# Transposed copies of x and adj loaded in 32x32 blocks, and attention's products with v issued in pairs

## The chip, the cores and the metric

The kernel runs on one core of a Trainium2 chip. The metric is the device time of one execution in microseconds (us). TensorE (PE in the profile, its weight loads PEld), VectorE (DVE), ScalarE (ACT), GpSimd (POOL) and SyncE (SP) each run their own instructions in order; 16 DMA engines move data. Here DMAs are issued by SP and, in a few places, by ACT.

## The reference

32 independent graphs, each with x[512, 256] and a 0/1 matrix adj[512, 512], pass through four layers. In all of them `x = layernorm(x + layer(x, adj))`.

```
layer 0: q, k, v = x@Wq+bq, x@Wk+bk, x@Wv+bv          (8 heads of 32)
         s = q @ k.T / sqrt(32); s = where(adj > 0, s, -9e15)
         out = (softmax(s) @ v) @ Wo + bo
layer 1: relu(((1+eps)*x + adj@x) @ W1 + b1) @ W2 + b2              (hidden 512)
layer 2: silu(rmsnorm((eps*x + adj@x) @ W1 + b1)) @ W2 + b2         (hidden 1024)
layer 3: softplus(xn@W_self + (I - s_out*adj*s_in) @ xn @ W_neigh), xn = layernorm(x)*gamma + beta
```

`s_out` and `s_in` are the inverse square roots of adj's column and row sums. All is float32.

## The kernel before

**The planner.** `graph(b)` does not issue instructions. It notes operations: an engine, a cost in ns, a function that issues the instructions, the tiles read and written. `Order` (L53 to L261) then makes one list of all 32 graphs' operations. It runs a model in which each engine takes, among the operations that could start soonest, the one with the smallest due time (`run`, L100); a graph's due times are shifted by `PERIOD` for each graph (`emit`, L240). `slot_time` (L135) keeps an operation back until its buffers are free: each tile tag has a fixed number of buffers. A DMA from SP occupies the queue for its `issue` time and lands `lat` (2000 by default) after its cost. The functions are called in the list's order, so the order on each engine is fixed before the program runs; the model's costs have no other effect. Two graphs overlap: the late layers of one run beside the attention of the next.

**Loads and transposes.** For each graph SP loads x (`xs`, one buffer, L374) and adj (`ad`, one buffer, L377) with rows on partitions. Matrix products need both with the other axis on partitions. TensorE transposes 128x128 blocks into PSUM: 16 for adj (L556; ACT copies the result to `adjT`, two buffers, and sums the out-degrees on the way, L563), 8 for x (L585; VectorE or ACT copies to `xT`, one buffer, L590). `bias` (bfloat16, L573) is 0 where adj is set and a huge negative number elsewhere. `adjT` is used from the first aggregation (L1037) to the Laplacian (L1299); its diagonal is kept in `diag0` (L952) and altered for layers 1 and 2. The row sums `d_in` are made by VectorE from `ad` (L964).

**Attention** (`attend`, L666). Heads go in two groups of four. For each of four row tiles of 128 queries:

- TensorE forms the scores of four heads (row-tiled products, L680) in PSUM.
- Per head, VectorE adds `bias`, negates, takes the row minimum, and writes to `pr` (three buffers, L699); ACT computes the exp of `pr` into `pq` (two buffers, L713), in a permuted order of columns, with the row sum.
- VectorE transposes all 32x32 blocks of `pq` in place (128x2048, L728).
- 16 DMAs of 64 KB move quarters of partitions to `pT` (two buffers, L739). SP issues them; in the first graph ACT shares them.
- TensorE multiplies with v, 32 column-tiled products (`pv`, L777) into `po_att`, one quarter of its columns per row tile.

A group ends by scaling with the reciprocal row sums (L796 to L848). The other layers are products (L863, L1037, L1054, L1258, L1299) with elementwise work between them.

Of the kernel before, what the change touches and what calls it, by code (L numbers as in the profile page):

```python
# [11 lines left out]
AF = mybir.ActivationFunctionType  # L12
ALU = mybir.AluOpType
# [3 lines left out]
P = 128  # L17
NEG = -9007199254740992.0
LN_EPS = 1e-5
RMS_EPS = 1e-6  # L20
HEADS = 8
PERIOD = 70000
LEAD = {}


# [27 lines left out]
class Order:  # L53
# [46 lines left out]
    def run(self, ops, key, back=False):  # L100
# [32 lines left out]
        done, out = set(), []  # L133

        def slot_time(o):  # L135
            t = 0.0
            for x in o.bufs:
                if not x.taken:
                    s = slots.setdefault(x.slot, [0.0] * x.bufs)
                    if not s:  # L140
                        return None
                    t = max(t, min(s))
            return t

        while len(out) < len(ops):
            best = None
            for e, lst in cand.items():
# [3 lines left out]
                for c in lst:  # L151
# [4 lines left out]
                    t = max(free[e], o.ready, st)  # L156
                    way = o.ways[c[3]]
                    if e == "DVE" and "port" in way[3] and pool_busy[0] <= t < pool_busy[1]:
                        t = pool_busy[1]
# [18 lines left out]
                x = min((x for x in opts if x[0] <= t_min + self.WINDOW), key=lambda x: x[1])  # L178
# [8 lines left out]
            t, e, c = best  # L187
# [22 lines left out]
            for x in o.bufs:  # L210
                if not x.taken:
                    x.taken = True
                    s = slots[x.slot]
# [51 lines left out]
def kernel(  # L265
# [29 lines left out]
    nc = tc.nc  # L295
    B, N, D = x.shape
    NT = N // P
    DC = D // P
    HD = D // HEADS
    HPG = P // HD  # L300
# [11 lines left out]
    ident = const.tile([P, P], F32, name="ident")  # L312
# [167 lines left out]
    def graph(b):  # L480
        first, last = b == 0, b == B - 1
        def op(ways, r=(), w=(), hold=()):
            order.op(b, ways, r, w, hold, stage[0])
# [3 lines left out]
        def bank(name):  # L487
            return Buf(ps, [P, 512], F32, "m", f"{name}_{b}", 4)

        def tmp(shape, tag, bufs, name=None, dtype=F32):  # L490
            return Buf(sb, shape, dtype, tag, f"{name or tag}_{b}", bufs)

        def pe(cost, fn, r, w, *hold, turn="whole"):

            op([("PE", cost, fn, {"turn": turn})], r, w, hold)

        def dve(cost, fn, r, w, port=False):
            op([("DVE", cost, fn, {"port": 1} if port else {})], r, w)
# [10 lines left out]
        def evacuate(dst, src, r, w):  # L509
            either(  # L510
                r, w,
                (690, lambda: nc.vector.tensor_copy(dst(), src())),
                (590, lambda: nc.scalar.copy(dst(), src())),
            )
# [17 lines left out]
        def small(name, bufs=2, shape=None):  # L532
            return Buf(sb, shape or [P, NT], F32, "s_" + name, f"{name}_{b}", bufs)
# [12 lines left out]


        stage[0] = "adjT"
        adjT = tmp([P, NT, N], "adjT", 2)
        d_out, d_in = small("d_out"), small("d_in")  # L550
        for m in range(NT):
            pt = bank("pt_adj")

            def tr_adj(m=m, pt=pt):
                for t in range(NT):
                    nc.tensor.transpose(  # L556
                        pt[:, t * P : (t + 1) * P], ad[:, t, m * P : (m + 1) * P], ident
                    )

            pe(460, tr_adj, [(ad,)], [(pt,)], adjT, d_out)  # L560
            act(
                675,
                lambda m=m, pt=pt: nc.scalar.activation(  # L563
                    adjT[:, m, :], pt(), AF.Identity, accum_out=d_out[:, m : m + 1]
                ),
                [(pt,)], [(adjT, m), (d_out, m)],
            )
        allT = [(adjT, m) for m in range(NT)]

        bias = tmp([P, NT, N], "bias", 1, dtype=BF16)  # L570
        dve(
            1250,
            lambda: nc.vector.tensor_scalar(  # L573
                bias(), ad(), scalar1=0.0, scalar2=NEG, op0=ALU.is_le, op1=ALU.mult
            ),
            [(ad,)], [(bias,)], port=True,
        )
        stage[0] = "xT"
        xT = tmp([P, DC, N], "xT", 1)
        for c in range(DC):  # L580
            pt = bank("pt")

            def tr_x(c=c, pt=pt):
                for t in range(NT):
                    nc.tensor.transpose(  # L585
                        pt[:, t * P : (t + 1) * P], xs[:, t, c * P : (c + 1) * P], ident
                    )

            pe(460, tr_x, [(xs,)], [(pt,)], xT)
            evacuate(lambda c=c: xT[:, c, :], pt, [(pt,)], [(xT, c)])  # L590
        y = tmp([P, NT, D], "y_att", 2)
        pool(
            2400,
# [10 lines left out]
        def qk(m):  # L604
            stage[0] = "qk"
            for w, w_k, dst, bias_c, bias_k, scale in (
                (wq, "wq", qT, bqs_c, "bqs_c", QK_SCALE),
                (wk, "wk", kT, bk_c, "bk_c", 1.0),
            ):
                pq = bank("pq")  # L610

                def mm(w=w, pq=pq):
                    for c in range(DC):
                        nc.tensor.matmul(  # L614
                            pq(),
                            lhsT=w[:, c, m * P : (m + 1) * P],
                            rhs=xT[:, c, :],
                            start=(c == 0),
                            stop=(c == DC - 1),
                        )  # L620

                pe(1720, mm, xTc + [(w_k,)], [(pq,)], dst)
                col = bias_c[:, m : m + 1]
                either(
                    [(pq,), (bias_k,)], [(dst, m)],
                    (
                        750,
                        lambda dst=dst, pq=pq, col=col, scale=scale: nc.vector.tensor_scalar(
                            dst[:, m, :], pq(), scalar1=scale, scalar2=col,
                            op0=ALU.mult, op1=ALU.add,  # L630
                        ),
                    ),
                    (
                        680,
                        lambda dst=dst, pq=pq, col=col, scale=scale: nc.scalar.activation(
                            dst[:, m, :], pq(), AF.Identity, bias=col, scale=scale
                        ),
                    ),
                )
# [26 lines left out]
        def attend(g):  # L666
# [2 lines left out]
            mx = small("mx", 2, [P, NT, HPG])  # L669
            rs = small("rsum", 2, [P, NT, HPG])  # L670
            po = bank("po_att")
            for t in range(NT):
                stage[0] = "scores"

# [18 lines left out]
                pq = tmp([P, 4, HPG, NT, 32], "pq", 2)  # L693
                for j in range(HPG):

                    pr = tmp([P, N], "pr", 3)
                    dve(
                        780,
                        lambda t=t, j=j, sc=sc, pr=pr: nc.vector.tensor_tensor_reduce(  # L699
                            out=pr(),  # L700
                            in0=sc[:, j, :],
                            in1=bias[:, t, :],
                            scale=-1.0,
                            scalar=3.0e38,
                            op0=ALU.add,
                            op1=ALU.min,
                            accum_out=mx[:, t, j : j + 1],
                        ),
                        [(sc, j), (bias,)], [(pr,), (mx, t, j)],
                    )  # L710
                    act(
                        800,
                        lambda t=t, j=j, pr=pr, pq=pq: nc.scalar.activation(  # L713
                            pq[:, :, j].rearrange("p a c s -> p c a s"),
                            pr().rearrange("p (c a s) -> p c a s", a=4, s=32),
                            AF.Exp,
                            bias=mx[:, t, j : j + 1],
                            scale=-1.0,
                            accum_out=rs[:, t, j : j + 1],
                        ),  # L720
                        [(mx, t, j), (pr,)], [(pq, j), (rs, t, j)],
                        table="exp",
                    )
                stage[0] = "move"
# [6 lines left out]
                    ),  # L731
                    [], [(pq, j) for j in range(HPG)], port=True,
                )
                pT = tmp([P, 4, HPG, NT, 32], "pT", 2)

                def move(queue, to, pq=pq, pT=pT):
                    for a in to:
# [24 lines left out]
                else:  # L762
# [5 lines left out]
                        pqk, [(pT, a) for a in range(4)],  # L768
                    )

                stage[0] = "pv"
                def pv(t=t, pT=pT):

                    for c in range(NT):
                        for j in range(HPG):
                            h = g * HPG + j
                            nc.tensor.matmul(  # L777
                                po[j * HD : (j + 1) * HD, t * P : (t + 1) * P],
                                lhsT=v[:, c, h * HD : (h + 1) * HD],
                                rhs=pT[:, :, j, c, :],  # L780
                                start=(c == 0),
                                stop=(c == NT - 1),
                            )

                pe(
                    1060, pv, [(pT, a) for a in range(4)] + [(v, c) for c in range(NT)],
                    [(po,)], oT, turn="col",
                )

# [622 lines left out]
```

## Time and profile before

| | |
|---|---|
| median of 3 runs | 3604.89 us (3603.01 to 3605.39) |
| profiled execution: its time, its span | 3604.95 us, 3603.2 us |
| granted TensorE clock, mean | 0.989 |
| PE busy | 3501.9 us (97%), 20616 products |
| VectorE busy | 2902.0 us (81%) |
| ScalarE busy | 1836.2 us (51%) |
| GpSimd busy | 854.7 us (24%) |
| DMA engines' time, SP's queue | 36.5%, 253440 packets |
| DMA engines' time, ACT's queue | 0.4%, 2304 packets |
| moves `pT<-pq` from SP | 4048 of 64 KB, 2.0 us to landing |
| loads of adj, of x | 32 of 1024 KB, 5.8 us; 32 of 512 KB, 4.0 us |

A line of a group gives the kernel line, engine, operation, output and inputs by the program's names, shapes, count; then busy us and the mean ns of one; then the idle time just before and what ended it. A line of waits gives who waited for whom, us in total, how often, the longest. A line of the chain gives start, length, and what ran or was waited for; the chain is followed back from the last instruction.

### The profile page before, as it was taken

How to read it: one execution, taken by the hardware profiler on the slowest of the kernel's cores; microseconds unless marked ns; L12 is line 12 of the kernel's file. 1: busy time of each engine (PE TensorE's matmuls, PEld its weight loads, DVE VectorE, ACT ScalarE, POOL GpSimd, SP SyncE). 2: the span in 40 equal slices, each digit the busy share in tenths (PEclk: the TensorE clock that was granted, in tenths of full speed). 3: DMA queues.
4: the chain of work that ended last, by engine and by line, in shares of the span. 5: the costliest groups of instructions: out<-in, count | busy, mean ns of one | idle time of the engine just before them, and what ended most of it. 6: DMA issues, size and time to landing. Idle time of an engine off the chain costs nothing.

```text
span 3603.2 us, 60546 instructions
## 1 busy us (share of the span) xinstructions
PE 3501.9 (97%) x20616; PEld 2086.9 (58%) x20616; DVE 2902.0 (81%) x6458; ACT 1836.2 (51%) x3591; POOL 854.7 (24%) x614
## 2 busy tenths in 40 slices
PE   6899999999999999999999999999999999999897
PEld 3455565665565665555655555655656655656464
DVE  6778888888888888887888888888888888887855
ACT  3445554545554545555455555455545455544533
POOL 1112222222222122222122222122222222221221
PEclk8999999999999999999999999999999999999998
DMA  6434333334333333333333333343333343333410
GB/s 174 115 91 109 93 99 100 94 88 106 98 102 97 91 96 101 99 100 93 94 99 98 100 99 95 92 101 100 98 99 95 87 106 99 101 97 79 100 30 12
DMA packets 256052, 344.82 MB, mean 96 GB/s; under 512 B 71552, under 2 KB 107776, under 8 KB 255744
## 3 DMA queue, kind: packets, MB, share of 16 engines
q1 hardware_dynamic: 253440, 337.79, 36.5%
q10 hardware_dynamic: 2304, 3.15, 0.4%
q8 instruction: 165, 2.70, 0.3%
q14 instruction: 143, 1.17, 0.1%
HBM read 55.46 MB, written 16.78 MB: 20 GB/s over the span
## 4 chain that ended last, share of the span: by engine, by line
PE 82%; ACT 5%; SPq 5%; DVE 2%; issue 2%; DMA 1%; ACTq 0%; POOL 0%; DVEq 0%; POOLq 0%
PE po L863 21%; PE ph L1037 11%; PE pg L1054 10%; PE sc L680 6%; PE pa L1054 6%; PE pz L1258 6%; PE pq L614 6%; PE pa_l L1299 6%; SPq L739 5%; PE po_att L777 5%; PE pv L650 3%; ACT L1349 1%; PE pt L585 1%; PE pt L1230 1%; PE pt_adj L556 1%
## 5 line engine op out<-in xcount | busy, mean ns | idle before, releaser
L713 ACT ACTIVATE pq<-pr,mx 128x512 f32<-128x512 f32 x1024 | 729.0, 713 | 437.6 <-DVE mx L699 203.9
L699 DVE CUSTOM_DVE_ANT_0 pr<-sc,bias 128x512 f32<-128x512 f32 x1024 | 665.0, 684 | 205.2 <-PE sc L680 172.7
L728 DVE STREAM_TRANSPOSE pq<-pq 128x2048 f32<-128x2048 f32 x256 | 590.5, 2307 | 41.9 <-ACT pq L713 30.6
L863 PE MATMUL po<-w,gT 128*128 128x256 f32 x2048 | 478.6, 385 | 5.2 <-ACT gT L1193 5.2
L1054 PE MATMUL pg<-hT,w 128*128 128x512 f32 x1024 | 470.8, 599 | 2.2 <-DVE gT L1109 1.1
L863 PEld LDWEIGHTS po<-w,gT 128*128 128x128 f32 x2048 | 387.0, 191 | 111.7 <-issue 54.9
L916 POOL TENSOR_TENSOR rstd<-ve,nhalf 128x4 f32<-128x4 f32 x132 | 132.4, 1003 | 1286.4 <-DVE ve L911 1280.5
L520 POOL TENSOR_TENSOR ssq<-ssq,sq 128x512 f32<-128x512 f32 x219 | 279.4, 1276 | 211.8 <-ACT sq L1130 205.1
L1054 PEld LDWEIGHTS pg<-hT,w 128*128 128x128 f32 x1024 | 187.1, 190 | 235.0 <-issue 212.7
L777 PE MATMUL po_att<-pT,v 128*32 128x128 f32 x8192 | 281.2, 279 | 32.7 <-DMA pT<-pq 22.7
L680 PE MATMUL sc<-kT,qT 32*128 32x512 f32 x2048 | 298.1, 652 | 9.2 <-DVE mx L699 9.2
L777 PEld LDWEIGHTS po_att<-pT,v 128*32 128x32 f32 x8192 | 211.7, 110 | 157.2 <-issue 119.2
L1037 PE MATMUL ph<-adjT,y 128*128 128x512 f32 x512 | 242.9, 599 | 0.1
L1037 PE MATMUL ph<-adjT,y_att 128*128 128x512 f32 x512 | 239.8, 593 | 0.9 <-DVE y L877 0.9
L1054 PE MATMUL pa<-hT,w 128*128 128x512 f32 x512 | 236.3, 605 | 0.0
L863 PE MATMUL po<-w,aT 128*128 128x256 f32 x1024 | 234.6, 382 | 0.0
L1258 PE MATMUL pz<-wsn,xnT 128*128 128x512 f32 x512 | 230.8, 602 | 0.9 <-DVE xnT L1241 0.4
L1299 PE MATMUL pa_l<-zy,adjT 128*128 128x256 f32 x1024 | 227.6, 380 | 1.3 <-DVE zy L1310 1.3
L1299 PEld LDWEIGHTS pa_l<-zy,adjT 128*128 128x128 f32 x1024 | 194.1, 190 | 42.7 <-issue 15.3
L863 PEld LDWEIGHTS po<-w,aT 128*128 128x128 f32 x1024 | 189.7, 190 | 46.2 <-issue 21.9
L563 ACT ACTIVATE adjT<-pt_adj 128x512 f32<-128x512 f32 x128 | 75.2, 590 | 253.9 <-PE pt_adj L556 252.8
L520 POOL TENSOR_TENSOR sp<-sp,y 128x1024 f32<-128x1024 f32 x31 | 73.1, 2358 | 551.6 <-ACT sp L1349 551.5
(141 smaller groups left out, 5251.1 us busy)
## 6 DMA issues: line engine op xcount, KB each, us to landing
pT<-pq SPq DMA_DIRECT2D x4048, 64.0 KB, 2.0
adj<-in_adj_dram SPq DMA_DIRECT2D x32, 1024.0 KB, 5.8
x<-in_x_dram SPq DMA_DIRECT2D x32, 512.0 KB, 4.0
out_dram<-sp SPq DMA_DIRECT2D x31, 512.0 KB, 3.0
pT<-pq ACTq DMA_DIRECT2D x48, 64.0 KB, 2.2
w<-in_L_gnn_W_dram SPq DMA_DIRECT2D x2, 1024.0 KB, 8.2
w<-in_L_gnn_W_dram SPq DMA_DIRECT2D x2, 512.0 KB, 5.9
out_dram<-sp SPq DMA_DIRECT2D x2, 256.0 KB, 2.1
```

The source lines that it names most:

```text
L520: lambda: nc.gpsimd.tensor_tensor(dst(), dst(), src(), ALU.add), {},
L614: nc.tensor.matmul(pq(), lhsT=w[:, c, m * P : (m + 1) * P], rhs=xT[:, c, :], start=(c == 0), stop=(c == DC - 1),)
L680: nc.tensor.matmul(sc[:, j, :], lhsT=qT[hp, g, t * P : (t + 1) * P], rhs=kT[hp, g, :], start=True, stop=True,)
L699: lambda t=t, j=j, sc=sc, pr=pr: nc.vector.tensor_tensor_reduce(out=pr(), in0=sc[:, j, :], in1=bias[:, t, :], scale=-1.0, scalar=3.0e38, o ...
L713: lambda t=t, j=j, pr=pr, pq=pq: nc.scalar.activation(pq[:, :, j].rearrange("p a c s -> p c a s"), pr().rearrange("p (c a s) -> p c a s", ...
L728: lambda pq=pq: nc.vector.transpose(pq().rearrange("p a j c s -> p (a j c s)"), pq().rearrange("p a j c s -> p (a j c s)"),),
L777: nc.tensor.matmul(po[j * HD : (j + 1) * HD, t * P : (t + 1) * P], lhsT=v[:, c, h * HD : (h + 1) * HD], rhs=pT[:, :, j, c, :], start=(c == 0),
L863: nc.tensor.matmul(po[:, i * D : (i + 1) * D], lhsT=lhs[:, k, t * P : (t + 1) * P], rhs=w[:, k, :], start=(i == 0 and k == 0), stop=(i == ...
L1037: nc.tensor.matmul(ph(), lhsT=xin[:, m, c * P : (c + 1) * P], rhs=adjT[:, m, :], start=(m == 0), stop=(m == NT - 1),)
L1054: nc.tensor.matmul(pa(), lhsT=w[:, c, m * P : (m + 1) * P], rhs=hT[:, c, :], start=(c == 0), stop=(c == DC - 1),)
L1258: nc.tensor.matmul(pz(), lhsT=xnT[:, c, t * P : (t + 1) * P], rhs=wsn[:, c, :], start=(c == 0), stop=(c == DC - 1),)
L1299: nc.tensor.matmul(pa[:, i * D : (i + 1) * D], lhsT=adjT[:, m, t * P : (t + 1) * P], rhs=zy[:, m, D : 2 * D], start=(m == 0), stop=(m == N ...
```

## The change

- **Blocks in place of TensorE's transposes.** x and adj are loaded a second time, straight into `xT` and `adjT`, by four DMAs each that ACT issues. Each fills 32 partitions, in pieces of 32 elements (128 B): 2048 pieces for a quarter of adj, 1024 for one of x. VectorE then transposes all 32x32 blocks in place, two operations of 128x1024 for adj and one for x. ACT's pass over `adjT` stays, for the out-degrees, but reads and writes `adjT` in SBUF. The plan counts 600 ns for an issue and 6000 (adj) or 4000 ns (x) until it lands. TensorE's 24 transposes a graph and `xT`'s copies from PSUM go; the first loads of x and adj stay.
- **The copy of the scores.** VectorE writes `bias` minus scores directly into `pq`, and ACT's exp works in place. `pr` goes. The permutation that the exp made is now in `kT` (its copy from PSUM reads permuted) and in `bias` (four operations instead of one, permuted).
- **Pairs.** `pv` is issued for two row tiles at a time, after the second one's move: 64 products in a run. `pT` has three buffers instead of two.
- The planner can give two buffers of one tag to one operation, and `PERIOD` is 72000 instead of 70000.

```diff
-PERIOD = 70000
+PERIOD = 72000
...
+        def load_blocks(dst, src, q):
+            v = src.rearrange("(i r) (m a c) -> a r m i c", r=32, a=4, c=32)
+            nc.scalar.dma_start(dst[32 * q : 32 * q + 32].rearrange("r m (i c) -> r m i c", c=32), v[q])
...
+        for q in range(4):
+            op(
+                [("ACT", 600, lambda q=q: load_blocks(adjT(), adj[b], q), {"lat": 6000})],
+                [], [(adjT, m, q) for m in range(NT)],
+            )
+        for m0 in range(0, NT, 2):
+            dve(
+                1200,
+                lambda m0=m0: nc.vector.transpose(
+                    adjT[:, m0 : m0 + 2].rearrange("p m i -> p (m i)"),
+                    adjT[:, m0 : m0 + 2].rearrange("p m i -> p (m i)"),
+                ),
...
-            pe(460, tr_adj, [(ad,)], [(pt,)], adjT, d_out)
             act(
                 675,
-                lambda m=m, pt=pt: nc.scalar.activation(
-                    adjT[:, m, :], pt(), AF.Identity, accum_out=d_out[:, m : m + 1]
-                ),
+                lambda m=m: nc.scalar.activation(
+                    adjT[:, m, :], adjT[:, m, :], AF.Identity, accum_out=d_out[:, m : m + 1]
+                ),
...
+        bias_v = lambda t: bias[:, t].rearrange("p (a c s) -> p c a s", a=4, c=4)
+        adj_v = lambda t: ad[:, t].rearrange("p (c a s) -> p c a s", a=4, c=4)
...
-            pe(460, tr_x, [(xs,)], [(pt,)], xT)
-            evacuate(lambda c=c: xT[:, c, :], pt, [(pt,)], [(xT, c)])
+        for q in range(4):
+            op(
+                [("ACT", 600, lambda q=q: load_blocks(xT(), x[b], q), {"lat": 4000})],
+                [], [(xT, c, q) for c in range(DC)],
+            )
+        dve(
+            1200,
+            lambda: nc.vector.transpose(
+                xT().rearrange("p c i -> p (c i)"), xT().rearrange("p c i -> p (c i)")
+            ),
...
+                if dst is kT:
+                    to = lambda: kT[:, m, :].rearrange("p (a c s) -> p c a s", a=4, c=4)
+                    src = lambda pq=pq: pq().rearrange("p (c a s) -> p c a s", a=4, c=4)
...
-                    pr = tmp([P, N], "pr", 3)
+                    row = lambda pq=pq, j=j: pq[:, :, j].rearrange("p a c s -> p a (c s)")
                     dve(
                         780,
-                        lambda t=t, j=j, sc=sc, pr=pr: nc.vector.tensor_tensor_reduce(
-                            out=pr(),
-                            in0=sc[:, j, :],
-                            in1=bias[:, t, :],
+                        lambda t=t, j=j, sc=sc, row=row: nc.vector.tensor_tensor_reduce(
+                            out=row(),
+                            in0=sc[:, j, :].rearrange("p (a n) -> p a n", a=4),
+                            in1=bias[:, t, :].rearrange("p (a n) -> p a n", a=4),
...
-                            pq[:, :, j].rearrange("p a c s -> p c a s"),
-                            pr().rearrange("p (c a s) -> p c a s", a=4, s=32),
-                            AF.Exp,
+                            row(), row(), AF.Exp,
...
-                pT = tmp([P, 4, HPG, NT, 32], "pT", 2)
+                pT = tmp([P, 4, HPG, NT, 32], "pT", 3)
+                pTs.append(pT)
...
+                if t % 2 == 0:
+                    continue
                 stage[0] = "pv"
-                def pv(t=t, pT=pT):
-                    for c in range(NT):
+                two = [(t - 1, pTs[t - 1]), (t, pT)]
+                def pv(two=two):
+                    for t, pT, c in [(t, pT, c) for t, pT in two for c in range(NT)]:
...
-                    1060, pv, [(pT, a) for a in range(4)] + [(v, c) for c in range(NT)],
+                    1960, pv,
+                    [(pT, a) for _, pT in two for a in range(4)] + [(v, c) for c in range(NT)],
```

## The prediction, made before the result was known

> **What bounds the kernel now.** I read the windows first, for one period of the steady state (a graph's `pt` transposes to the next graph's: 1036.4 to 1145.35 us, 108.95 us; the next period has the same length). Columns: length, then busy time of PE, PEld, DVE, ACT and POOL with the instructions of each, then the granted clock, the DMA share and GB/s.
>
> ```profile
> 1036.40:1145.35 108.95, 108.43 (x644) 64.75 (x644) 90.18 (x202) 57.36 (x112) 26.91 (x20) 1.00 0.38 97
> 1145.35:1254.30 108.95, 108.43 (x644) 64.74 (x644) 90.16 (x202) 57.35 (x112) 26.91 (x20) 1.00 0.38 97
> ```
>
> PE is busy for 108.43 of 108.95 us at the full granted clock; DVE has 18.8 us of idle time, ACT 51.6, the DMA engines 62%. So a microsecond taken from PE shortens the period, as long as nothing else fills up. Then the chain of waits over the same stretch (start, us, what), to see what PE pays for transposes and for the products with v:
>
> ```profile
> 1036.40 0.04 issue
> 1036.44 1.09 PE pt L585 x8
> 1037.53 1.72 PE pg L1054 x4
> ...
> 1078.64 1.01 PE po_att L777 x32
> 1079.66 1.92 PE po L863 x8
> ...
> 1089.73 1.72 PE ph L1037 x4
> 1091.45 1.73 PE po L863 x8
> ...
> 1134.13 0.44 PE pt_adj L556 x4
> 1134.57 1.72 PE ph L1037 x4
> ```
>
> Four whole-array products take 1.72 to 1.73 us, but 1.92 right after a column-tiled `po_att` group: leaving that mode costs 0.19. Third, who waits (who, for whom, us in total, times, longest):
>
> ```profile
> ACT pq L713 <- DMA pT<-pq: 149.6, 34, 8.1
> ...
> PE po_att L777 <- DMA pT<-pq: 22.7, 11, 5.9
> ...
> PE pt L585 <- ACT gT L1115: 13.5, 26, 0.5
> ```
>
> and the same for SP's DMA queue:
>
> ```profile
> SPq L377 <- PE pt_adj L556: 272.9, 29, 10.2
> SPq L739 <- DVE pq L728: 169.8, 93, 5.8
> ```
>
> PE hardly waits for the moves (22.7 us in the whole run, 11 times); the wait for a move's read of `pq` stands on ACT; SP stands 272.9 us in front of the adj load, for PE's last transpose.
>
> **What the change takes from PE**, per graph.
> - adj transposes: 16. Eight are two lots of 0.44 us in the chain; the other eight run from 1029.33 to 1030.30 in PE's timeline (0.97). 1.85 us.
> - x transposes: 8. `po_att` ends at 1035.92 and `pt` at 1037.53: 1.61 us, of which 0.52 is the wait for ACT. The 0.19 for leaving the column mode, which falls in there, passes to the next product. 1.42 us.
> - Products with v in pairs: 8 column groups become 4 of double length. Leaving costs 0.19 (above). Entering: a whole 128x512 product takes 0.43, so 128 columns 0.107, and 32 of them four abreast 0.86; the group takes 1.01, so 0.15. A dropped group saves 0.19 to 0.34; I take 0.30, nearer the upper end since 0.86 is worked out from the same rows. Four: 1.2 us (0.76 to 1.36).
>
> Together 4.5 us (4.0 to 4.6): the period would be 104.45, and 32 x 4.5 = 144 us come off. The profiled execution took 3604.95 us (span 3603.2 and 1.75 around it), 0.06 from the median of the runs, 3604.89. The floor is thus about **3461**.
>
> **What it adds to the others**, per graph.
> - DVE: transposes. A 128x2048 one takes 2307 ns (L728), so three 128x1024 ones 3.46 us.
> - DVE: xT's copies from PSUM go, 57 of 64 on DVE at 0.69: -1.2 us.
> - DVE: the bias is four 512-element operations with 32-element runs in place of one of 1233 ns (L573). This form is not in the trace. At best each takes a quarter of 1233 ns and nothing changes; at worst 745 ns, as 512 elements from PSUM do (L1078), +1.75. I take 0.5 us each (L934 needs 0.41 for 256 elements): +0.8.
> - DVE: the score operation writes four runs of 128 in `pq` instead of one of 512. Zero, or at worst the 55 ns by which the strided TENSOR_TENSOR L1019 (728) exceeds L877 (673): 32 x 55 = 1.8. I take 0, because strided and dense forms of one kind lie within 8%. The exp has 713 ns, as the 624 of L1130 (SBUF too) plus the 90 that a bias adds elsewhere (L1115's 674 against 587 for a copy); its strided output seems to have cost nothing, so the dense one gains nothing. kT's permuted read: zero likewise, at most 55 ns twice.
> - Sum for DVE: 90.17 + 3.46 - 1.2 + 0.8 = 93.2 (92.4 to 95.9), 89% of 104.45.
> - ACT: 8 DMA issues at 0.60 us (ACT's own moves in the first graph): 57.4 + 4.8 = 62.2. adjT's pass from SBUF instead of PSUM costs some 40 ns each; hidden by 42 us of idle time.
> - SP: nothing is added. 128 move issues at a pitch of 0.632 us are 80.9 us, 77% of the new period. Its 8.5 us a graph in front of the adj load go, since no PE transpose reads that buffer any more; what is late next there is DVE's degree sum (L964).
> - DMA: 12288 pieces of 128 B. The trace's packet records have no such size: 4 B take 9 ns, 1024 B from HBM 46. On the line between them 128 B take 13.5 ns; the ends are 9 and 46. 12288 x 13.5 / 16 engines = 10.4 us (6.9 to 35), so the DMA share goes from 0.38 to 0.50.
>
> The row at 1024 B is full speed per byte (16 x 1024 B in 46 ns), and 128 B at 13.5 ns is 43% of that. The Trainium skill (DMA: Bandwidth & Descriptors, Specifications) speaks against such pieces: at least 512 B are needed for line rate, and below it the engine reads, modifies and writes. If each 128 B piece cost what 512 B do on my line (27 ns), the 10.4 us would be 21, and the load of adj would take 14 us instead of 7 on idle engines. The same skill (VectorE: DVE Perf Modes, The three transpose paths) has 390 ns for a 128x128 bf16 transpose on TensorE and 311 on VectorE; by it the trade is 9.4 us off PE for 7.5 on DVE. The trace's float32 rows are 0.11 in a run and 2307/16 = 144 ns, and they decide.
>
> **What is given back.** In-order waits:
> - The blocks land late. An adj quarter is 128 packets an engine, 1.7 us alone and about 3 beside the moves; four and the 2.0 us of any landing make 10 to 14 us from the first issue, where the plan has 2.4 + 6. x: 5 to 8 against 6.4. VectorE stands at the transpose for the difference, if the plan put it there that early.
> - DMAs use eight semaphores in turn, SP's and ACT's together, and each waits until the DMA eight before it has landed (the waits in the trace's DMA instructions show it; in the first graph ACT lost 5.4 us at 31 to 37 us so, while x and adj came in). A block load issued behind a move of 16 waits for that move's ninth DMA: up to 9 x 0.632 + 2.0 = 7.7 us on ACT, with the exps queued behind it. The moves issued after the loads wait for the loads on SP: about 7 us for adj, 3 for x.
> - The score operation now writes `pq` itself, so the 149.6 us of ACT's waits for moves (4.7 a graph) pass to DVE.
>
> Against this stands PE's cover: over 24 tiles in three graphs, `po_att` started 4.6 to 21 us after its move had landed, and in pairs the first tile has more. Each of the two sets a graph costs PE what exceeds that: 0 for most, a few us where cover is 5. I take 0.65 a set, 1.3 a graph, 41 us. At the start PE's first products wait for x until 4.91 us and for Wq until 8.29; the blocks share full DMA engines there and need a VectorE transpose (1.2 us) more, for which I take 3 us (0 to 8). **Forecast: 3461 + 41 + 3 = 3505** (3460 to 3550), 50%.
>
> **Rivals.**
> - VectorE becomes the bound, 18%. Now it waits 172.7 + 137.5 + 113.0 = 423 us for PE's scores, `ph` and `pa_l`, 13.2 a graph. If these stay and busy time is 94.5, the period is 107.7 and the gain 1.25 x 32 = 40: **3565** (3550 to 3597). For it: 89% busy and new waits at its head; against: those waits shrink when DVE is late.
> - SP is held by the blocks, and it is slower: 28%. SP has 80.9 + 1.5 (loads, store) of 108.95, and 12.4 us of waits for DVE and PE at the moves today (169.8 + 115.5 + 56.9 + 55.2 over 32). Its moves can lose 14 us a graph by the semaphores before the period is back at 109. With packets of 27 ns, in the middle between the bounds 9 and 46, adj lands about 7 us later and x 3, and the 7 + 3 that the moves lose above become 17 or more: 3 x 32 = 96 us more, **3700** (3612 to 3850). For it: SP is a serial queue at 77%; against: the 12.4 us of waits would be absorbed first.
> - The change moves the waits and nothing else, 4%: **3605**. PE would wait 4.5 us a graph at `po_att`, eight times 0.5; only a narrow band of delays gives this.
>
> **Numbers.** A measurement of this kernel can tell 0.2% (7 us) from no change. Faster 0.50 + 0.18 = 0.68, the same 0.04, slower 0.28. The range 3450 to 3665 holds the forecast and its rivals down to the lighter part of the slower one; 2 in 10 lie outside, nearly all above. The forecast's own range is 3460 to 3550.
>
> **What would show it.** In a steady period: length 105.9; PE busy within 2 us of it; no `pt_adj`, no `pt` from x; `po_att` groups of 64 in about 1.9 us; DVE near 93 us; DMA share 0.50, 128 B packets near 13.5 ns; waits of PE for `pT` below 70 us in total. I am wrong if PE's idle time before `po_att` is over 3 us a graph, if SP's moves wait for adjT's loads by over 14 us a graph, if 128 B packets take 25 ns or more, or if DVE is over 95% busy.

## The result: 3704 us, 2.9% slower, and the profile after

The changed kernel takes 3703.81 us (median of 4 runs, 3699.99 to 3716.75) against 3604.01 for the kernel before on the same chip: ratio 1.0285, 95% interval [1.0273, 1.0298]. The forecast was 3505, the range 3450 to 3665. The profiled span is 3700.9 us (3603.2 before).

**A lap** below is the time from one graph's first `pa_l` product to the next graph's; the windows of before ran from one graph's `pt` to the next's, which has the same length. "Start" is the time until the second graph's first `pa_l`, the lap a mean over the next 26, "end" the rest of the span.

| | start | lap | end | span |
|---|---|---|---|---|
| before | 363.1 | 108.95 | 407.5 | 3603.2 |
| after | 403.9 | 110.87 | 414.5 | 3700.9 |
| difference | +40.8 | 26 x 1.92 = +49.9 | +7.0 | +97.7 |

The windows of after, over two laps (same columns as before):

```profile
1070.50:1180.40 109.90, 105.97 (x621) 62.50 (x620) 95.60 (x208) 53.49 (x108) 27.79 (x20) 1.00 0.45 110
1180.40:1290.90 110.50, 106.51 (x622) 62.46 (x621) 95.95 (x208) 53.09 (x108) 27.82 (x20) 1.00 0.46 111
```

PE did lose work, 108.43 to some 106.2 us, but now stands idle 4 us a lap where it stood 0.5. VectorE is at 87%: no new bound. The laps, equal before, now differ (109.6 to 112.8).

PE's part of the timeline of after in the second of these laps (start, us, then engine, line, operation; in brackets the idle time just before and who ended it):

```profile
1199.93 1.98 PE L1081 MATMUL pg<-hT,w 128*128 128x512 f32 x4 [0.24 <-DVE gT L1136]
...
1207.00 1.95 PE L803 MATMUL po_att<-pT,v 128*32 128x128 f32 x64
...
1231.36 3.72 PE L890 MATMUL po<-wo,oT 128*128 128x256 f32 x16
1236.57 10.63 PE L890 MATMUL po<-w,gT 128*128 128x256 f32 x48 [1.49 <-ACT gT L1220]
```

The pairs work: 64 products in 1.95. But the last product waits 1.49 us for ACT's silu (L1220). Why the silu is late stands in ACT's timeline of the same stretch, and a second such place in its timeline 45 us earlier:

```profile
1187.54 5.97 ACTq L553 DMA_DIRECT2D adjT<-in_adj_dram  x4
1193.64 1.06 ACT L1360 ACTIVATE sp<-zy 128x1024 f32<-128x1024 f32 x1 [8.76 <-DMA adjT<-in_adj_dram]
```

```profile
1230.40 0.69 ACT L657 ACTIVATE kT<-pq,bk_c 128x512 f32<-128x512 f32 x1 [0.62 <-PE pq L631]
1232.68 0.60 ACTq L553 DMA_DIRECT2D xT<-in_x_dram  x1
1233.31 1.28 ACT L1220 ACT_TABLE_LOAD   x1 [2.23 <-DMA pT<-pq]
1233.38 1.62 ACTq L553 DMA_DIRECT2D xT<-in_x_dram  x2
1234.61 1.91 ACT L1220 ACTIVATE gT<-gT 128x2048 f32<-128x2048 f32 x1
1235.04 0.76 ACTq L553 DMA_DIRECT2D xT<-in_x_dram  x1
1236.42 1.90 ACT L1220 ACTIVATE gT<-gT 128x2048 f32<-128x2048 f32 x1
```

The ACTq lines are DMA issues: ACT stands in them, four for adj in 5.97 us. The first x load stands in front of the silu's table load. ACT is free at 1231.09, when its copy to `kT` ends, but this load's issue starts only at 1232.68 and takes 0.60: of the 2.23 us before the table load, 1.6 are a wait of the load itself, and what ended it, by the profile, is the landing of a move (`DMA pT<-pq`). The waits of after, over the whole run, with the same columns as before; first PE, then the others:

```profile
PE po L890 <- ACT gT L1220: 57.4, 29, 4.6
PE sc L703 <- DVE mx L722: 39.0, 10, 12.6
PE pg L1081 <- DVE gT L1136: 30.0, 29, 2.6
...
PE po_att L803 <- DMA pT<-pq: 12.3, 11, 3.8
```

```profile
ACT pq L736 <- DMA pT<-pq: 240.7, 30, 18.1
...
ACT sp L1360 <- DMA adjT<-in_adj_dram: 168.3, 19, 10.1
...
ACT L1220 <- DMA pT<-pq: 69.9, 27, 4.9
```

```profile
DVE pq L722 <- DMA pT<-pq: 148.1, 102, 7.1
...
DVE adjT L565 <- DMA adjT<-in_adj_dram: 29.4, 16, 7.7
```

```profile
SPq L761 <- DVE pq L749: 126.2, 72, 7.9
...
SPq L761 <- DMA adjT<-in_adj_dram: 77.5, 110, 2.4
```

`po_att` waits less than before (12.3 against 22.7). What PE waits for is new: the silu and `gT`. As foretold, VectorE now waits for the moves itself (148.1 us, 102 times); but the wait did not leave ACT, whose exps still wait for them, 240.7 us by the profile (149.6 before). SP's wait for the adj blocks is 77.5 us, 2.4 a graph.

At the start, ACT's timeline shows 12 block loads in its queue ahead of its first copy, until 27.82 us:

```profile
0.74 7.69 ACTq L553 DMA_DIRECT2D xT<-in_x_dram  x4
9.00 18.82 ACTq L553 DMA_DIRECT2D adjT<-in_adj_dram  x8
27.91 1.28 ACT L657 ACT_TABLE_LOAD   x1 [27.91 <-DVE self L420]
29.20 0.69 ACT L657 ACTIVATE qT<-pq,bqs_c 128x512 f32<-128x512 f32 x1
```

In the first 100 us PE is busy for 45.29 us, before for 65.36. The granted clock is lower at the start too: 0.89 on the mean until 403.9 us, against 0.94 until 363.1 us in the kernel before. In the 26 laps it fell to half in six stretches of 3.4 us, 20.5 us in all, and in none before; PE was busy in all of them, so at most 10 of the 49.9 us are a slower clock.

**Where a lap's time went on PE.** The time from each product's start to the next product's start, added up by tile and divided by 26 laps, in us. A wait counts to the product ahead of it. (Two experiments stand beside them; they are told below.)

| tile of the product | before | after | no_block_loads | quarter_tr |
|---|---|---|---|---|
| `pt_adj`, `pt` from x | 2.73 | 0 | 0 | 0.79 |
| `po_att` | 8.68 | 7.76 | 7.89 | 9.11 |
| `po` from wo (then the silu's product) | 3.56 | 5.48 | 3.56 | 3.56 |
| `pg` | 14.04 | 15.33 | 14.04 | 14.04 |
| `pv` | 3.64 | 4.72 | 4.75 | 3.65 |
| all others | 76.30 | 77.58 | 77.74 | 76.51 |
| lap | 108.95 | 110.87 | 107.98 | 107.66 |

### The profile page after: what moved, and what is told of

Same layout as the page of the kernel before. It is cut to its first block, busy times and chain, and to the rows that moved or that the text cites. A ratio compares the mean times of both kernels' runs of the same rounds, so it can differ in the third digit from the quotient of the medians.

```text
span 3700.9 us, 59395 instructions
## 1 busy us (share of the span) xinstructions
PE 3450.1 (93%) x19848; PEld 2024.0 (55%) x19848; DVE 3070.5 (83%) x6655; ACT 1715.4 (46%) x3466; POOL 879.0 (24%) x614
## 5 line engine op out<-in xcount | busy, mean ns | idle before, releaser
L736 ACT ACTIVATE pq<-pq,mx 128x512 f32<-128x512 f32 x1024 | 727.6, 712 | 783.1 <-DVE mx L722 409.0
L722 DVE CUSTOM_DVE_ANT_0 pq<-sc,bias 128x512 f32<-128x512 f32 x1024 | 655.4, 684 | 198.2 <-DMA pT<-pq 148.1
L890 PEld LDWEIGHTS po<-w,gT 128*128 128x128 f32 x2048 | 394.8, 194 | 151.5 <-ACT gT L1220 69.7
L803 PE MATMUL po_att<-pT,v 128*32 128x128 f32 x8192 | 260.3, 278 | 13.3 <-DMA pT<-pq 12.3
L890 PE MATMUL po<-w,aT 128*128 128x256 f32 x1024 | 227.1, 380 | 0.7 <-DVE aT L1105 0.7
L969 ACT ACTIVATE y<-y,nmr,rstd 128x256 f32<-128x256 f32 x151 | 81.4, 592 | 263.4 <-DVE nmr L950 263.4
```

The costliest lines, as they stand in the source:

```text
L722: lambda t=t, j=j, sc=sc, row=row: nc.vector.tensor_tensor_reduce(out=row(), in0=sc[:, j, :].rearrange("p (a n) -> p a n", a=4), in1=bias[ ...
L736: lambda t=t, j=j, row=row: nc.scalar.activation(row(), row(), AF.Exp, bias=mx[:, t, j : j + 1], scale=-1.0, accum_out=rs[:, t, j : j + 1],),
L803: nc.tensor.matmul(po[j * HD : (j + 1) * HD, t * P : (t + 1) * P], lhsT=v[:, c, h * HD : (h + 1) * HD], rhs=pT[:, :, j, c, :], start=(c == 0),
L890: nc.tensor.matmul(po[:, i * D : (i + 1) * D], lhsT=lhs[:, k, t * P : (t + 1) * P], rhs=w[:, k, :], start=(i == 0 and k == 0), stop=(i == ...
```

## The experiments

The expectations name their theories by letters. My theory at first was H: ACT is held by the block loads. Against it stood D, the small pieces of 128 B, and V, VectorE, which is fuller and waits for the moves itself. Later came Q, the dropped copy and the in-order waits that it brings; O, that any new order of the planner costs something; L, that the loads cost most of what was lost; F, that TensorE's time is the period; and N, that time saved on TensorE turns into waits. The planner writes a new order when one of its inputs changes, so each run says whether its order is that of before, that of after, or a new one.

**The order of after, loads issued elsewhere or in other pieces.**

```diff
-            nc.scalar.dma_start(dst[32 * q : ...], v[q])
+            nc.sync.dma_start(dst[32 * q : ...], v[q])      (issue_sp)
+            nc.gpsimd.dma_start(dst[32 * q : ...], v[q])    (issue_pool)
```

> The changed kernel with one word altered: SP issues the block loads instead of ACT; the planner's list, and so the order on every engine, stays (in the plan the loads still cost ACT 600 ns). Theory H (ACT is held: it stands 6 us at each set of adj loads and 28 us at the start, with exps, silu and PSUM copies behind) expects most of the loss back: start 30 us shorter, PE's wait for the silu (57 us in all) gone, 3600 to 3650 us. Theory V (VectorE is too full: 95.6 of 110.5 us busy) and theory D (128 B packets crowd out the moves) expect 3690 to 3710, and the moves on SP held by 6 us more for each set could make it worse.

Measured: 4078.32 us, ratio 1.132 [1.1303, 1.1336]. Neither branch of the expectation held. On SP, in the same plan, the loads stand behind the moves and land late. The waits of this run:

```profile
DVE adjT L565 <- DMA adjT<-in_adj_dram: 277.7, 29, 11.1
...
PE pg L1081 <- DVE gT L1136: 262.2, 28, 10.8
```

A late block stops VectorE, in order, and `gT` behind it, and PE behind that. This is what a late landing costs; a part of it is the clock (granted 0.94 on the mean, 0.98 in after).

> The changed kernel with one word altered: GpSimd issues the block loads, on its own queue; same list of operations. Under theory H the result is at least as good as with SP, since neither ACT nor the moves' queue stands behind a load, unless GpSimd needs long for 2048 pieces: at over 5 us an issue its sums (ssq, residuals, rsqrt) come late and PE waits for them: 3560 to 3640 us if issues are short, over 3750 if they are long. Theories V and D expect 3690 to 3710.

Measured: 3669.76, ratio 1.0188 [1.0173, 1.0203], 34 us less than after (ratios 1.0285 and 1.0188). PE's waits of this run:

```profile
PE pg L1081 <- DVE gT L1136: 64.5, 29, 3.2
PE sc L703 <- DVE mx L722: 48.6, 12, 14.9
```

The wait for the silu is no longer among the large ones (3.0 us in all); the one for `gT` has doubled, from 30.0 us. One cause went and the other grew. The start is 395.1, 9 us less than after.

> The changed kernel with the same eight loads a graph, of the same bytes into the same tiles from ACT, but in pieces of 1024 B instead of 128 B (256 and 128 packets a load instead of 2048 and 1024). This leaves the block layout out: the tiles hold rows of x and adj in the wrong places, so its output is not the reference's. Theory D expects nearly all of the loss back (below 3560 us). Theory H expects the part back that comes from long issues (1.3 to 2.2 us each become 0.6), the start above all: about 3620 to 3670, and the part that comes from ACT's waits for the moves' semaphores stays. Theory V expects 3690 to 3710.

```diff
-            v = src.rearrange("(i r) (m a c) -> a r m i c", r=32, a=4, c=32)
+            v = src[128 * q : 128 * q + 128].rearrange("(r k) (h n) -> r (k h) n", k=4, n=256)
...
```

Measured: 3661.72, 1.0165 [1.0150, 1.0180]. PE's waits:

```profile
PE sc L704 <- DVE mx L723: 50.3, 12, 20.6
PE po L891 <- ACT gT L1221: 46.2, 27, 3.4
```

The mirror image: the silu's wait stays, the one for `gT` is 1.1 us in all. An x load's issue is 0.35 us here (median), and still ACT stands in front of the silu's table load nearly as long as in after (69.9 us):

```profile
ACT L1221 <- DMA pT<-pq: 60.4, 27, 4.1
```

So it is not the length of the issue that holds the silu, but the load's wait for an earlier move to land. Theory H's expectation had named this part as the one that would stay.

> The changed kernel, same order, with the block loads issued by GpSimd and in pieces of 1 KB in place of 128 B; what lands in adjT and xT is not the blocks, so the values are not the reference's. If ScalarE's issue (34 us by the run with GpSimd) and the small pieces (42 us by the run with 1 KB) are two causes that add: 3625 to 3635, neither the wait for the silu nor that for gT is left. If they overlap: 3650 to 3665.

Both edits together: 3604.60, 1.0006 [0.9998, 1.0015]; start 390.1, lap 108.09. The two together take 99 us off, more than 34 + 42 = 76 and more than either branch of the expectation. On GpSimd alone the wait for `gT` had doubled (64.5 us); with the larger pieces as well, 8.7 us of it are left, and 3.4 of the silu's.

> The changed kernel with the block loads left out: VectorE transposes the first graph's adj and x as loaded and, later, the weights of one layer, so the values are not the reference's; a copy on ScalarE takes the absolute value to keep sums positive. Every engine else has the changed kernel's order and work. Theory L (the loads, by issue on ScalarE, transfer and landing, cost most of what was given back): 3600 to 3640 us, the second lap at 370 (404 in the changed kernel), the period at most 109.5. Theory V (the order, VectorE's transposes and the dropped copy cost it): 3670 or more, period over 110.

```diff
-            nc.scalar.dma_start(dst[32 * q : ...], v[q])
+            pass
...
-                    adjT[:, m0 : m0 + 2].rearrange("p m i -> p (m i)"),
+                    ad[:, m0 : m0 + 2].rearrange("p m i -> p (m i)") if first else w11.rearrange("p c f -> p (c f)"),
```

Measured: 3596.07, 0.9974 [0.9965, 0.9983]; start 380.0, lap 107.98. Two laps in its windows:

```profile
1025.30:1132.90 107.60, 105.73 (x622) 62.68 (x621) 96.07 (x208) 53.31 (x108) 27.96 (x20) 1.00 0.37 98
1350.90:1458.30 107.40, 105.68 (x622) 62.61 (x621) 96.02 (x208) 53.30 (x108) 27.88 (x20) 1.00 0.37 98
```

With VectorE's work and every order unchanged, the loads alone are worth 108 us: 24 at the start, 26 x 2.9 = 75 in the laps, 6 at the end. In the laps of after, PE's waits for the silu (45.6) and for `gT` (26.2) add up to 71.8; here both are gone. So nearly all that the block loads cost in the laps is these two waits.

**The order of after, changed.** The planner's PERIOD back to 70000 (after_p70), a move planned at 10100 instead of 8900 ns (move101), and loads planned on GpSimd at 1000 ns with 12 and 8 us to landing (pool_planned):

> The changed kernel with the PERIOD of 70000 of the kernel before. Theory O: it differs from the changed kernel's 3704 us by over 0.5%, either way. If order matters little: 3685 to 3720. In both the first laps are as late as in the changed kernel, some 40 us behind the kernel before, since the first loads do not change.

> The whole change, but the planner counts 10100 ns for the 16 issues of a move instead of 8900; 16 x 0.632 us is what they take. Only the order of operations differs. If VectorE's and PE's new waits come from moves that end 1.2 us later than the plan says, VectorE's 148 us of waits for moves and PE's waits shrink, and the time falls to 3620 to 3680 us; if not, it stays at 3690 to 3720.

> The changed kernel with the block loads issued by GpSimd, planned there at 1000 ns each with 12 us (adj) and 8 us (x) until they have landed, in place of 600 ns on ScalarE with 6 and 4 us. If wrong durations in the plan were what cost the loads their gain: 3600 to 3630, period at most 108.5. If a new order costs 1 to 1.5% by itself, as in the two plans tried on the kernel before: 3650 to 3690.

Measured: 3742.97, 1.0395 [1.0381, 1.0409]; 3855.72, 1.0705 [1.0687, 1.0723]; 3680.36, 1.0223 [1.0208, 1.0239]. The same work, between 2.2 and 7% above the kernel before. As theory O had it, after_p70 differs from after by over 0.5%, and pool_planned lies in the range given to a new order. In move101 PE waits for `oT` above all:

```profile
PE po L890 <- DVE oT L875: 167.3, 26, 8.2
PE sc L703 <- DVE mx L722: 70.6, 34, 14.5
```

I had expected a truer cost of the moves to help; it hurt (in part by the clock, granted at 0.956 on the mean against 0.980 in after). A plan told the issue time and landing of the loads did not make the change pay either.

**The same on the kernel before.** PERIOD 72000 (before_p72), a move at 10100 (before_mv), nothing else:

> The kernel before with the planner's PERIOD of 72000 in place of 70000 and nothing else: the same operations in another order. Theory O: 1 to 3% slower, with PE idle in many places of 0.3 to 1 us. Theory Q, and that the orders are about as good as each other: within 0.5% of the kernel before, 3590 to 3620 us.

> The kernel before with the planner's cost of a move at 10100 in place of 8900 ns and nothing else, the same step that cost the changed kernel 4%. Theory O: 1 to 5% slower (3640 to 3780 us). If the kernel before has slack that the changed one lacks: within 0.5%, 3590 to 3620.

Measured: 3658.68, 1.0151 [1.0137, 1.0165], and 3642.26, 1.0109 [1.0095, 1.0122]. A new order with the same operations costs 1.1 to 1.5% here. Theory O holds: a difference of this size between two kernels with different orders says nothing about the edit. The runs with new orders are to be read so:

> The changed kernel without the block loads: TensorE transposes x and adj as before; products with v in pairs, no copy of the scores, planner as in the change. If the blocks alone are the loss, this is faster than the kernel before by the pairs' share, 32 x 0.9 to 1.3 us: 3560 to 3580 us. Theory V (VectorE now waits for the moves' buffers itself, 148 us in all) expects part of the loss here: 3605 to 3660 us.

> The kernel before with one part of the change: the copy of the scores dropped (score operation writes pq, exp in place, kT and bias permuted). No pairs, no blocks. Theory Q (in-order VectorE now waits for the move that reads pq, where ACT waited before and pr's three buffers let VectorE run on) expects most of the loss of the pairs-and-no-copy kernel (period 111.1 us) here: 3640 to 3680 us. Rival P (the pairs are the loss: the second tile's move is waited for and moves bunch) expects 3600 to 3610.

> The same with three buffers for pq instead of two, so that the score operation needs a buffer whose move ended a tile earlier. Theory Q expects VectorE's wait for the moves to vanish (below 15 us in all) and the time to return to 3600 to 3615 us. If it does not, the loss of the dropped copy lies in the order that the planner makes, or in the permuted operations.

> The kernel before with only the block loads and VectorE's transposes in place of TensorE's. PE loses 3.3 us of work a graph. Theory H expects the start to be 30 us longer (ACT issuing loads for 28 us), and a steady period of 107 to 109 us: 3570 to 3640 us in all, so that the blocks are not the main loss. If the blocks are the main loss in this setting too, above 3660.

> The kernel before, copy kept and products not in pairs; x and adj in blocks as in the change, but issued by GpSimd in place of ScalarE, in the same plan as the run with the blocks alone (3705). If ScalarE's issue time and its queue cost the blocks their gain: 3600 to 3650. If not: within 1% of 3705, above 3670.

> The kernel before, copy kept, products with v not in pairs, adj by TensorE; only x is loaded a second time in blocks, issued by GpSimd, and transposed by VectorE. TensorE saves 1.4 us a graph. Theory F with loads that land in time: 3560 to 3580. Theory O (a new order costs 1 to 1.5%, whatever the operations): 3600 to 3630. Theory L: 3640 or more.

| run | what of the change it has | us | ratio | start | lap |
|---|---|---|---|---|---|
| pairs_nocopy | pairs, dropped copy | 3670.56 | 1.0195 [1.0178, 1.0212] | 368.8 | 111.15 |
| nocopy | dropped copy | 3677.98 | 1.0207 [1.0191, 1.0222] | 377.8 | 111.18 |
| nocopy_pq3 | dropped copy, `pq` in three buffers | 3625.49 | 1.0061 [1.0046, 1.0076] | 364.6 | 109.57 |
| blocks | block loads | 3705.07 | 1.0283 [1.0268, 1.0299] | 403.5 | 110.73 |
| blocks_pool | block loads issued by GpSimd, plan of blocks | 3690.95 | 1.0243 [1.0229, 1.0257] | 389.1 | 110.76 |
| xblocks_pool | blocks of x alone, GpSimd | 3667.15 | 1.0178 [1.0164, 1.0192] | 384.5 | 110.62 |

None of these is faster than the kernel before, and the parts do not add (2.07 + 2.83 is over 2.85). Pairs alone were not run. Those with block loads start late by 21 to 40 us; those without by 2 to 15. From blocks to blocks_pool, in one plan, the median falls by 14 us and the start by as much (403.5 to 389.1), the lap not at all: on this order ACT's queue costs something only while the first graphs come in. Of the expectations, nocopy fell in Q's range, blocks above its mark for the blocks as the main loss (3660), blocks_pool on its branch "if not", xblocks_pool in L's range. pairs_nocopy missed both ranges, V's by 11 us, and nocopy_pq3 missed Q's: 10 us above it, with 32.3 us of VectorE's waits for the moves in place of less than 15. With new orders none of them decides between theories.

**The order of before, one thing changed.** nocopy_same drops the copy (with the permuted `kT` and `bias` that go with it) but leaves the planner's notes as they were, so every engine keeps its order:

```diff
                     pr = tmp([P, N], "pr", 3)
+                    row = lambda pq=pq, j=j: pq[:, :, j].rearrange("p a c s -> p a (c s)")
...
-                            out=pr(),
+                            out=row(),
...
                         [(sc, j), (bias,)], [(pr,), (mx, t, j)],
```

> The kernel before with only the scores' copy dropped, and with the planner still told of the old copy, so that every engine keeps the order of the kernel before; only what the score operation writes changes. Theory Q (VectorE, in its order, now waits for the move that reads pq, in place of ScalarE): 3650 to 3690 us, and VectorE waits for pT's DMAs at the score operation for over 100 us in all. Theory O (the loss of the variant without the copy came from the new order that the planner wrote for it): 3600 to 3620, VectorE's waits below 60.

Measured: 3664.74, 1.0169 [1.0155, 1.0183]. VectorE's waits:

```profile
DVE pq L708 <- PE sc L688: 136.2, 89, 3.6
...
DVE pq L708 <- DMA pT<-pq: 112.3, 57, 7.5
```

The copy did protect VectorE's order: Q holds. But the lap is only 109.39 (+0.44, 12 us in all), and 28.3 of the 112.3 us lie there. The start is 32 us longer and the end 17. The windows of the two starts (before, then nocopy_same) tell what the 32 are:

```profile
0.00:363.10 363.10, 313.70 (x1966) 178.69 (x1967) 279.03 (x610) 166.97 (x363) 67.74 (x54) 0.94 0.47 122
0.00:395.30 395.30, 329.84 (x1966) 185.87 (x1967) 277.79 (x622) 167.03 (x363) 68.01 (x54) 0.89 0.43 112
```

PE has the same 1966 products in both. Half of the 32 us is idle time (49.4 to 65.5), and half is that the same products are busy 16.1 us longer, at a granted clock of 0.89 in place of 0.94. What lowers the clock no run tests; the dropped copy is the only change here.

quarter_tr leaves one transpose in place of four:

```diff
-                for t in range(NT):
+                for t in range(1):
                     nc.tensor.transpose(
...
-                    adjT[:, m, :], pt(), AF.Identity, ...
+                    adjT[:, m, :].rearrange("p (t q) -> p t q", q=P),
+                    pt[:, 0:P].unsqueeze(1).to_broadcast([P, NT, P]), AF.Identity, ...
```

> The kernel before with one 128x128 transpose in place of four for each block row of x and adj; ScalarE's and VectorE's copies read that one four times over, so the values are not the reference's, but every engine has the same operations in the same order. 18 transposes of 0.11 us leave TensorE in a graph, 2.0 us. Theory F (TensorE's time is the period, as the forecast took it): 32 x 2.0 = 63 us less, 3541 (3530 to 3555), period 107.0. Theory N (others are due just behind TensorE, and its saving turns into waits): 3580 or more, period over 108.2.

Measured: 3566.35, 0.9899 [0.9885, 0.9912], lap 107.66. Between the two theories: 1.94 us less of transposes a lap, as priced, and 1.29 off the lap. Over the laps, the waits of this run, and under them those of before:

```profile
PE pt L587 <- ACT gT L1121: 23.7, 25, 1.0
PE po_att L783 <- ACT adjT L563: 4.0, 26, 0.2
```

```profile
PE pt L585 <- ACT gT L1115: 13.0, 25, 0.5
PE pg L1054 <- ACT gT L1115: 0.5, 1, 0.5
```

PE comes earlier and waits longer for the same releases. The clock has no part in it: in the laps of both kernels it never left 1.00.

## Why the prediction was wrong

**The price of the work was right.** Transposes taken from PE: 2.73 us a lap against 1.85 + 1.42, of which 0.52 was a wait for ACT. Pairs: 0.92 at `po_att`, that wait included, and 0.39 at `po` from aT, `pa` and `pr_r` (7.20, 7.26 and 0.62 before, 7.00, 7.17 and 0.52 after); without the wait some 0.8 to 0.9, where I had 1.2. Together 4.0 us a lap, at the lower end of my 4.0 to 4.6. Pieces of 128 B: ACT's queue takes 9.3% of 16 x 3700.9 us (0.4% of it moves) for 393216 pieces, 13.4 ns each; I took 13.5. The Trainium skill (DMA: Bandwidth & Descriptors, Specifications) asks for at least 512 B to reach line rate. The trace agrees that 128 B stay below it (13.4 ns, against 46 ns for 1024 B, is 43% of the rate per byte), but not with the 27 ns a piece that I had estimated with the page. The score operation still takes 684 ns, the bias 0.47 a quarter (0.5). VectorE's 95.6 to 96.0 us is in the range of 92.4 to 95.9 or just over.

**The step that failed is "What is given back", priced at 1.3 us a graph and 3 at the start.** Saved on PE in a lap are about 4.0 us; the lap grew by 1.92, so 5.9 came back, and 41 at the start.

- *"A block load issued behind a move of 16 waits for that move's ninth DMA: up to 7.7 us on ACT, with the exps queued behind it", covered at `po_att`.* The wait came, but the cover is not where the loads stand: ahead of the silu, which PE waits for. I followed the exps behind the loads and not the silu. In front of the silu's table load ACT stands 2.6 us (69.9 in 27 times), 0.6 of it the issue and the rest the load's wait for a move. Price: `po` from wo, 1.9 us a lap.
- *"8 DMA issues at 0.60 us" on ACT.* An issue of 2048 pieces takes 1.53 us (median), one of 1024 0.76: 9.2 us a graph. But this is not what made the silu late: the issue in front of it takes 0.60, as I had it, and in pieces_1k, where it takes 0.35, the silu's wait stays.
- *"VectorE stands at the transpose for the difference."* It does (29.4 us in all), and `gT` behind it is due at once: `pg`, 1.3 us a lap. I had looked for the cover only at `po_att`, where it held (12.3 us of waits in the run). Pieces of 1 KB, which shorten the issues and the landings alike, take this wait away; no run parts the two.
- *The start, 3 us (0 to 8)*: 41. ACT's 12 issues hold its first copies until 29.20 us; GpSimd's issue gives back 9, 1 KB pieces 11, both 14, leaving the loads out 24. The other 17 remain without any load; dropping the copy costs 32 there in the order of before. My 3 us were a delay of the first products alone; a granted clock of 0.89 in place of 0.94 up to the second lap had no term in the sum.
- *A microsecond off PE is one off the lap.* The floor of 3461 rested on this. quarter_tr: two thirds.
- *The order.* I took the new plan to be as good as the old. In no_block_loads, neither of the two load waits is there, and still only 0.97 of some 4.0 us reach the lap: `pv` has 1.1 us more, `sc` 0.7, and many places 0.2 to 0.3. Of these 3 us 1.4 are longer idle time of PE (1.96 us a lap against 0.53): `pm_t` and `pr_r` wait for VectorE 12.6 us each over the laps, `pm` for GpSimd 8.0, `pt` for VectorE 5.6. A slower clock is at most 0.3 (17.1 us of the laps at half). As for the cause: if quarter_tr carries over (a third of what PE saves is lost to releases that come no earlier), 1.3 of the 3 us are that, and by nocopy_same 0.4 are the dropped copy; the rest is not settled. Two harmless changes of the plan cost 1.4 and 1.7 us a lap.

**The rivals.** "SP is held by the blocks" gave 3700, and 3704 came, but not so: SP's moves waited 2.4 us a graph for the blocks where I had put the turning point at 14, and `po_att` stayed covered. Its number was right by chance. VectorE did not become the bound. The signs I had named as proof against me (`po_att`, SP, pieces, VectorE over 95%) all stayed quiet, since they watched the path I had thought of and not PE as a whole.

**Open**: how the 17 us at the start that need no load divide between the dropped copy and the order, how far each acts through the lower clock, and what lowers that; how much of the 3 us a lap is the order; and whether some order lets the change pay. Of all runs, those below the kernel before leave part of the work out, so there is no version here that beats it.

## What to carry to other kernels

When a change puts DMA issues on an engine that also computes, ask for each what it must wait for before it is issued, price the issue at its piece count, and look at the instruction behind it and at who waits for that one; the engine's idle share is no cover. Where a planner or a scheduler writes the order, keep the order fixed while testing an edit, and first measure what a harmless new order costs: here 1.1 to 1.5%, four tenths to a half of the 2.8% that the edit was meant to bring. A buffer that looks like a needless copy may be what lets an in-order engine run ahead of a DMA. Look at the granted clock of a stretch before putting its whole loss down to waits: at the start of nocopy_same the clock was half of it.

## What the runs showed of the hardware

The first issue of a set took 0.60 us on ACT, of 2048 pieces as of 1024. Those behind it take longer, and more so with more pieces: the four adj loads of one lap took 0.60, 1.32, 1.53 and 2.18 us, the four x loads of the lap shown above 0.60, 0.82, 0.77 and 0.76. The two lists below are the loads of after and of pieces_1k (least, median and most ns):

```profile
L553 ACTq DMA_DIRECT2D xT<-in_x_dram x128: 586/760/3855, 0.7 to 3341.9; - x128
L553 ACTq DMA_DIRECT2D adjT<-in_adj_dram x128: 594/1530/4176, 9.0 to 3551.3; - x128
```

```profile
L554 ACTq DMA_DIRECT2D xT<-in_x_dram x128: 317/352/1519, 0.7 to 3300.6; - x128
L554 ACTq DMA_DIRECT2D adjT<-in_adj_dram x128: 317/580/669, 4.4 to 3505.5; - x128
```

GpSimd took 1.25 us for a quarter of adj. The Trainium skill (DMA: Bandwidth & Descriptors, Issuing engine by pattern) calls the path of SyncE and ScalarE generally the faster one; for these loads, with 2048 pieces, GpSimd's issue was the shorter of the two (1.25 against 1.53), while the landing took longer (median 6.3 us for a quarter of adj against 5.6).
